# A four-layer graph network on one core: layers 1 to 3 as rounds of fixed order, and idle TensorE products in front of attention in layers 1 and 2

## The chip, the core and the metric

The kernel runs on one core of a Trainium2 chip. The metric is the device time of one execution in microseconds (us). TensorE is PE in the profile (PEld its weight loads), VectorE is DVE, ScalarE is ACT, GpSimd is POOL, SyncE is SP.

## The reference

There are 4096 nodes with 256 channels and a dense 0/1 adjacency matrix with about 9 neighbours a row, itself among them. Each of four layers adds an attention over a node's neighbours to the node's own row:

```python
h = np.maximum(layernorm(x), 0.0); x = x + L0(h)   # 8 heads, curvature bias, masked softmax
h = np.maximum(layernorm(x), 0.0); x = x + L1(h)   # 1 head: leaky_relu(a1.h_i + a2.h_j, 0.2)
h = np.maximum(layernorm(x), 0.0); x = x + L2(h)   # see below
h = np.maximum(layernorm(x), 0.0); x = x + L3(h)   # 4 heads of 64, see below
```

Layer 2 makes two softmaxes over the neighbours, of the scores e and of -e, applies both to `inp` (the second with a minus sign), concatenates the two results, multiplies them by `wtrans` (512x256) and applies elu. Layer 3 has dot-product scores `leaky_relu(h_n . h_m, 0.01)` per head; a pair that is not an edge has the score 1.0 instead of minus infinity, so that the softmax runs over all 4096 nodes, and the result goes through relu.

## The kernel before, in words

The nodes are 32 tiles of 128 rows. From the adjacency matrix the kernel builds, beside layer 0, a list of each tile's edges: 9 chunks (`EC`) of 128 slots, a slot holding the row number of one neighbour, and marks that say which of the tile's rows a slot belongs to. Layer 0 is ordered by a planner with due times; the change does not touch it.

For layers 1, 2 and 3 each layer first has a table in device memory (`table1`, `table2`, `table3`) with the transformed rows of all nodes, written two tiles at a time by `store_two` on ACT's DMA queue (L774). A tile's work in a layer is this:

- **Gather.** POOL issues one indirect DMA per chunk (L909) into one of 6 buffers `g` (`G`). Chunks 0 to 6 are early chunks (`gather_early`): they name only rows of tiles 0 to 27 and read only that part of the table, so that a layer's first gathers can start before the layer before has written its last four tiles. Chunk 7 is a late one (`gather_late`) and reads the whole table; in layer 2 chunk 8 is gathered in the same way. The tile's own rows (`SELF`) come by a DMA on SP's queue (L923).
- **Chunk 8 in layers 1 and 3** holds rows of tiles 28 to 31, and is not gathered: these four tiles' rows stay on the chip as three bf16 parts (`late_rows`, made by `keep_late`), and 12 products on PE pick from them (`expanded`, L1701).
- **Scores, weights, attention.** ACT makes exponentials and DVE multiplies the tile's 0/1 marks with them, giving the weight matrix `sw` (L1819 in layer 1, L1897 to L1906 in layer 2). PE sums the gathered rows with it (`summed`, L930, in layers 1 and 3; L1919, two halves of 14 products, in layer 2). In layer 3 the scores come from products of the marks with the tile's own rows (L2056), DVE multiplies them with the gathered rows (L2060), sums per head (L2061), and multiplies the rows with the weights (L2074); then `summed` uses the plain marks.
- **Afterwards.** Layer 1 adds the result to x, normalizes it and writes rows of `table2` (`finish1`, `rows2`). Layer 2 scales and transposes the two results (`signed2`, `turn_signed`), multiplies by `wtrans` (`through_wt`, L1954), applies elu, adds, normalizes (`finish2`), transposes (`turn3`), multiplies by layer 3's weights, and stores rows of `table3` and their three bf16 parts (`rows3`). Layer 3 divides, applies relu, adds and stores four tiles at a time.

The order comes from `run()` (L1714 on). Each step has a lag; the step of tile t with lag l is written down in round t + l. PE executes its instructions in exactly the order in which they are written down; for DVE, ACT, POOL and SP a scheduler chooses the order when the program is built. `begin` (the early gathers) has the lag 2 - G = -4. The late gathers of the first five tiles have lags of their own, so that at the start of a layer early gathers of four tiles come first, and `BEHIND` and `issue_after` keep POOL to this order:

```python
            def late_lag(t):
                return (-1, -2, -2, -3, -3)[t] if t < 5 else 2 - G
            steps = [(-3, loads), (2 - G, begin), (late_lag, begin_late)] + [
                (lag, lambda t, f=f: f(t, of[t])) for lag, f in steps
            ]
```

Of the kernel before, what the change touches and what calls it, by code (L numbers as in the profile page):

```python
# [20 lines left out]
P = 128  # L21
# [683 lines left out]
BEHIND = 3  # L705
ROW0, ROW1, ROW3 = C + H0 + CF, C + 2, C
# [7 lines left out]
def gnn_lists(  # L714
# [917 lines left out]
    with tc.tile_pool(name="work", bufs=2) as work, tc.tile_pool(name="kept", bufs=1) as kept:  # L1632
# [9 lines left out]
        mine1 = kept.tile([P, MINE, P + 3], BF16, name="mine1")  # L1642
        nc.gpsimd.tensor_copy(mine1[:, :, :P], ident_b[:, None, :].to_broadcast([P, MINE, P]))

        def by_edge(pool, t, st, own_t):

            my = mine1[:, t % MINE, :]
            nc.any.tensor_copy(my[:, P:], upper(own_t))
            s, parts = spread(pool.tile([P, 3, 512], F32, name="s_ps"), st, my, P + 3)
            a = work.tile([P, EC + 1], F32, name="a", bufs=3)  # L1650
            nc.vector.tensor_reduce(a[:, :EC].rearrange("p (b c) -> p b c", c=3), parts, AX.X, OP.add)
            return s, a
# [31 lines left out]
        def go_to(t, to):  # L1684

            pm = bank(ps_e, "pe")[:, :P]
            nc.tensor.matmul(
                pm, lhsT=col_late[:, t : t + 1].to_broadcast([P, P]), rhs=ident, start=True, stop=True
            )
            nc.vector.tensor_tensor(  # L1690
                to.rearrange("p (b e) -> p b e", b=LB), pm[:, None, :].to_broadcast([P, LB, P]),
                late_no[:, :, None].to_broadcast([P, LB, P]), op=OP.is_equal,
            )

        def expanded(t, of, width, pool, name):

            to = of.pop("to")
            ps = bank(pool, name)[:, :width]
            for b in range(LB):
                for i in range(3):  # L1700
                    nc.tensor.matmul(  # L1701
                        ps, lhsT=to[:, b * P : (b + 1) * P], rhs=late_rows[:, b, i, :width],
                        start=(b == 0 and i == 0), stop=(b == LB - 1 and i == 2),
                    )
            nc.scalar.copy(of["g"][:, LATE, :width], ps)
# [8 lines left out]
        def run(table, width, x_of, steps, first=None, expand=False, rows=True):  # L1714


            of, late = [{} for _ in range(NT)], {}

            def loads(t):
                two = t // 2 * 2  # L1720
                if t == two:
                    of[t]["ss"] = work.tile([P, 2, EC * P], BF16, name="ss", bufs=3)
                    if not first:
                        nc.sync.dma_start(of[t]["ss"], s_of[t // 2])
                of[t]["pair"] = of[two]["ss"]
                of[t]["s"] = by_slot(of[t]["pair"][:, t - two, :])
                if rows:
                    if t == two:
                        of[t]["sts"] = work.tile([P, 2, (EC + LB) * P], BF16, name="st", bufs=4)
                        if not first:  # L1730
                            nc.sync.dma_start(of[t]["sts"], rows_of[t // 2])
                    both = of[two]["sts"][:, t - two, :]
                    of[t]["st"], of[t]["to"] = both[:, : EC * P], both[:, EC * P :]
                if first:
                    marked(first, t, of[t]["st"])
                    go_to(t, of[t]["to"])
                    if t > two:
                        store(rows_of[t // 2], of[two]["sts"])
# [6 lines left out]
            def begin(t):  # L1745
                with ExitStack() as queue:
                    if t - BEHIND in late:
                        queue.enter_context(tc.issue_after(late.pop(t - BEHIND).ins))
                    of[t]["g"] = gather_early(t, table, width, g_pool)

            def begin_late(t):
                last = gather_late(t, of[t]["g"], table, width, range(EARLY, LATE if expand else EC))
                if t < G - BEHIND:
                    late[t] = last

            def late_lag(t):

                return (-1, -2, -2, -3, -3)[t] if t < 5 else 2 - G

            steps = [(-3, loads), (2 - G, begin), (late_lag, begin_late)] + [  # L1760
# [3 lines left out]
            for lag, f in steps:  # L1764
                for t in range(NT):
                    rounds.setdefault(t + (lag(t) if callable(lag) else lag), []).append((f, t))
            for r in sorted(rounds):
                for f, t in rounds[r] if r < NT else sorted(rounds[r], key=lambda s: -s[1]):
# [12 lines left out]
        with tc.tile_pool(name="only1", bufs=2) as only, tc.tile_pool(name="l1_o", bufs=2, space=PSUM) as ps_o, tc.tile_pool(  # L1781
# [10 lines left out]

            def expand1(t, of):
                expanded(t, of, ROW1, ps_e, "pe")

            def before1(t, of):
                s_ps, of["a"] = by_edge(ps_s, t, of["st"], own[0][:, t, :])
                nc.scalar.copy(three(of["s"]), s_ps)
                nc.scalar.copy(of["a"][:, SELF:], own[0][:, t, 0:1])
                if t % 2:  # L1800
                    store(s_of[t // 2], of["pair"])

            def give2(t, of):
                a, st = a2_of[:, t, :], of.pop("st")
                pm = bank(ps_m, "pm")[:, : EC * 3].rearrange("p (c s) -> p c s", c=EC)
                for c in range(EC):
                    nc.tensor.matmul(
                        pm[:, c, :], lhsT=st[:, c * P : (c + 1) * P], rhs=upper(own[1][:, t, :]),
                        start=True, stop=True,
                    )  # L1810
                nc.vector.tensor_reduce(a[:, :EC], pm, AX.X, OP.add)
                nc.scalar.copy(a[:, SELF:], own[1][:, t, 0:1])

            def weigh1(t, of):
                s = scores(of["g"], of.pop("a"))
                w = work.tile([P, EC + 1], F32, name="w")
                nc.scalar.activation(w, s, AF.Exp)
# [8 lines left out]
            def attend1(t, of):  # L1826
                sw, g = of.pop("sw"), of.pop("g")
                o = of["o"] = bank(ps_o, "o")[:, : C + 1]
                summed(o, sw, g, C + 1, [(sw[:, SELF, :], g[:, SELF, : C + 1])])

            def finish1(t, of):
# [7 lines left out]
                store_x(xs[1], t, of)  # L1839

            def rows2(t, of):
# [3 lines left out]
                for i, dst in enumerate((row[:, C + 1 :], own[1][:, t, 0:1])):  # L1845
# [3 lines left out]
                    )  # L1849
                if t % 2:  # L1850
                    store_two(table2, t, rows12[t // 2 % len(rows12)])
                split_own(own[1], t, 1)
# [4 lines left out]
                    (3, give2), (0, weigh1), (2, finish1), (1, attend1), (-1, before1),  # L1857
                    (2, rows2), (-1, expand1),
                ],
                first=only, expand=True,  # L1860
# [16 lines left out]
        with tc.tile_pool(name="only2", bufs=2) as only, tc.tile_pool(name="l2_o", bufs=2, space=PSUM) as ps_o, tc.tile_pool(  # L1877
# [5 lines left out]
            def weigh2(t, of):  # L1883

                s = scores(of["g"], a2_of[:, t, :])
                w = work.tile([P, EC + 1, 2], F32, name="w2")
                nc.scalar.activation(w[:, :, 0], s, AF.Exp)
                nc.scalar.activation(w[:, :, 1], s, AF.Exp, scale=-1.0)
                sw = of["sw"] = weights().rearrange("p (h c s r) -> p h c s r", h=2, s=2, r=HP)
# [22 lines left out]
            def attend2(t, of):  # L1912
                sw, g = of.pop("sw"), of.pop("g")
                of["o"] = []
                for h in range(2):
                    o = bank(ps_o, f"o{h}")[:, : C + 1]
# [6 lines left out]
                    of["o"].append(o)  # L1923

            def signed2(t, of):
                scale = small.tile([P, 2], F32, name="scale")
                two = of["two"] = only.tile([P, 2, C], F32, name="two")
                for h, o in enumerate(of["o"]):
                    nc.vector.reciprocal(inv[2][:, t, h : h + 1], o[:, :1])
# [3 lines left out]
                for h, o in enumerate(of.pop("o")):  # L1933
                    nc.scalar.activation(two[:, h, :], o[:, 1:], AF.Copy, scale=scale[:, h : h + 1])

            def turn_signed(t, of):
                two = of.pop("two")
                pt = bank(ps_t, "pt").rearrange("p (h k r) -> p h k r", h=2, k=KC)
# [3 lines left out]

                two_t = of["two_t"] = only.tile([P, 2, KC, 2, HP], F32, name="two_t")
# [13 lines left out]

            def finish2(t, of):
                pp, x = of.pop("pp"), of.pop("x")

                low = only.tile([P, C], F32, name="low")
                nc.vector.tensor_scalar(low, pp, 0.0, None, op0=OP.min)
                nc.scalar.activation(low, low, AF.Exp)
                nc.vector.scalar_tensor_tensor(low, pp, 0.0, low, op0=OP.max, op1=OP.add)
                nc.vector.scalar_tensor_tensor(x, low, -1.0, x, op0=OP.add, op1=OP.add)
                of["r"], of["rstd"] = normed(work, x)
                store_x(xs[2], t, of)
# [3 lines left out]
            def turn3(t, of):  # L1971
                of["hT"] = transposed(work, ps_t, of.pop("r"))

            def rows3(t, of):
                pp = times(ps_t, of.pop("hT"), w3_s, C)
                if t % 2 == 0:
# [4 lines left out]
                row, parts = (a[:, t % 2] for a in rows3_of)  # L1981
                nc.vector.scalar_tensor_tensor(
                    row, pp, of.pop("rstd"), b3_s, op0=OP.mult, op1=OP.add
                )
                if t % 2:
                    store_two(table3, t, rows3_of[0])
                    last3.append(rows3_of[0])
                rest = work.tile([P, C], F32, name="rest3")
                in_parts([parts[:, i, :] for i in range(3)], row, rest)
                if t % 2:  # L1990
                    store(own3[t // 2], rows3_of[1])
                nc.vector.tensor_add(all_rows, all_rows, row)
                sq = work.tile([P, D3], F32, name="sq")
                for k in range(K3):
                    nc.scalar.activation(
                        sq, row[:, k * D3 : (k + 1) * D3], AF.Square, accum_out=self3[:, t, k : k + 1]
                    )

# [3 lines left out]
                    (0, weigh2), (1, signed2), (2, finish2), (0, attend2), (2, turn3), (1, turn_signed),  # L2002
                    (2, rows3), (1, through_wt),
# [201 lines left out]
```

## Time and profile before

| | |
|---|---|
| median of 14 runs | 1612.54 us (1607.07 to 1617.04) |
| the profiled execution's own time | 1614.67 us |
| its span, first to last instruction | 1612.9 us |
| mean granted TensorE clock | 0.891 |
| busy: PE, DVE, ACT, POOL | 1289.6, 1148.0, 683.5, 1109.6 us |
| POOL's indirect DMAs | 1088, of which 288 in layer 0 |
| layer 1's gathers on POOL | from 530.03 us |
| layer 2's gathers | from 876.12 us |
| layer 3's gathers | 1249.85 to 1572.60 us |

A row of a timeline gives the start in us from the span's start, the duration, the engine, the line and operation, what it writes and reads, how many such were merged, and in brackets how long the engine had been idle and what released it. "ACTq" and "SPq" are DMA issues on those engines' queues. A row with several merged instructions gives the time from the first to the last. "issue" is idle time for which the profile shows no wait.

### The profile page before, as it was taken

The page shows a single profiled execution, that of the slowest core. Times are in us where ns is not written, and L with a number is a line of the kernel's source. Part 1 is how long each engine was busy: PE and PEld are TensorE (multiplying, and loading weights), DVE is VectorE, ACT ScalarE, POOL GpSimd, SP SyncE. Part 2 cuts the span into 40 slices and gives each one's busy share as a digit, 9 for nine tenths or more (in the row PEclk, how much of TensorE's full clock was granted, in tenths as well). Part 3 has the DMA queues.
Part 4 walks back from the last instruction along what each step waited for, and adds up shares of the span by engine and source line. Part 5 has one row for each costly group of instructions (what it writes and reads, how often), then busy time and mean ns, then how long its engine had stood idle before and what let it go on. Part 6 is the DMA issues. An engine that isn't in the chain of part 4 may idle for free.

```text
span 1612.9 us, 24838 instructions
## 1 busy us (share of the span) xinstructions
PE 1289.6 (80%) x7536; PEld 1032.9 (64%) x7536; DVE 1148.0 (71%) x3174; ACT 683.5 (42%) x1798; POOL 1109.6 (69%) x1179
## 2 busy tenths in 40 slices
PE   4673878877887679777777299988898789999995
PEld 2442655655665468665666288776777678888884
DVE  5666878888885567556555267666566599999995
ACT  4675767786452355434332044434334411211120
POOL 2127767776676677777777777777777777777770
PEclk9975888788998889888888599999999999999998
DMA  8978879997455668776768656666666667777740
GB/s 256 309 235 328 295 264 301 323 331 250 132 153 138 192 208 262 222 221 208 223 201 274 205 166 204 201 188 189 198 186 193 211 214 237 240 245 244 255 126 20
DMA packets 169888, 356.67 MB, mean 221 GB/s; under 512 B 32272, under 2 KB 104208, under 8 KB 169744
## 3 DMA queue, kind: packets, MB, share of 16 engines
q0 software_dynamic: 52224, 145.30, 32.4%
q1 hardware_dynamic: 67970, 143.98, 26.5%
q10 hardware_dynamic: 49550, 65.71, 11.4%
q8 instruction: 62, 1.02, 0.3%
q14 instruction: 82, 0.67, 0.1%
HBM read 291.66 MB, written 63.21 MB: 220 GB/s over the span
## 4 chain that ended last, share of the span: by engine, by line
PE 31%; DVE 17%; POOL 15%; DMA 11%; issue 9%; ACT 3%; DVEq 0%; ACTq 0%; POOLq 0%; SPq 0%
PE o L930 17%; POOL g L909 15%; DMA g<-table,nbr 10%; PE o L1919 4%; PE pv L2056 3%; DVE g L2074 2%; DVE sw L1897 2%; PE pv L1701 2%; PE pt L1954 2%; PE pt L874 1%; DVE g L1537 1%; PE pt L865 1%; DVE prod L1847 1%; DVE stats L842 1%; ACT mask L1204 1%
## 5 line engine op out<-in xcount | busy, mean ns | idle before, releaser
L909 POOL DMA_INDIRECT g<-table,nbr x1088 | 1080.2, 993 | 372.8 <-issue 295.9
L930 PE MATMUL o<-g,sw 128*128 128x257 f32 (+1 forms) x1216 | 313.5, 417 | 5.9 <-DVE sw L1822 5.9
L930 PEld LDWEIGHTS o<-g,sw 128*128 128x128 f32 x1216 | 252.6, 210 | 50.8 <-DVE sw L1822 6.6
L1919 PE MATMUL o<-g,sw 128*128 128x257 f32 x896 | 204.8, 386 | 27.0 <-issue 27.0
L1919 PEld LDWEIGHTS o<-g,sw 128*128 128x128 f32 x896 | 173.9, 194 | 53.8 <-issue 27.0
L930 PE MATMUL o<-g,s_f 128*128 128x264 f32 x576 | 152.8, 425 | 0.0
L930 PEld LDWEIGHTS o<-g,s_f 128*128 128x128 f32 x576 | 124.8, 217 | 27.5
L1204 ACT ACTIVATE mask<-adj,minus_half 128x1024 bf16<-128x1024 int32 x112 | 125.4, 1144 | 16.8 <-DMA adj<-in_adj_l 7.4
L2065 ACT ACTIVATE pm<-s 128x40 f32<-128x40 f32 x32 | 6.6, 208 | 227.2 <-DVE s L2063 219.9
L2056 PE MATMUL pv<-parts,st 128*128 128x256 bf16 x864 | 101.2, 275 | 1.4 <-DMA parts<-own 1.4
L2060 DVE TENSOR_TENSOR v<-pv,g 128x512 f32<-128x512 f32 (+1 forms) x160 | 90.7, 628 | 4.4 <-PE pv L2056 4.4
L2056 PEld LDWEIGHTS <-st 128*128 128x128 bf16 x864 | 85.1, 99 | 12.5 <-DMA parts<-own 1.8
L1954 PE MATMUL pt<-wt_s,two_t 128*128 128x256 f32 x256 | 69.5, 418 | 29.1 <-ACT two_t L1945 28.9
L2074 DVE SCALAR_TENSOR_TENSOR g<-pm,g 128x2560 f32<-128x2560 f32 x32 | 90.3, 2823 | 2.5 <-ACT g L2070 1.9
L1537 DVE TENSOR_TENSOR g<-g,pt 128x2560 f32<-128x2560 f32 x32 | 90.0, 2814 | 0.4 <-ACT pt L1534 0.3
L1701 PEld LDWEIGHTS <-st 128*128 128x128 bf16 x768 | 74.3, 98 | 13.8
L898 ACT ACTIVATE off<-place,minus 128x1152 bf16<-128x1152 f16 x64 | 80.0, 1249 | 6.6 <-DVE st L899 5.0
L2061 DVE TENSOR_REDUCE s<-v 128x36 f32<-128x2304 f32 x32 | 81.7, 2553 | 1.1
L865 PE MATMUL pt<-ident,r 128*128 128x128 f32 x192 | 42.8, 310 | 47.5 <-DVE r L845 35.7
L1954 PEld LDWEIGHTS pt<-wt_s,two_t 128*128 128x128 f32 x256 | 49.5, 203 | 45.9 <-ACT two_t L1945 39.6
L874 PE MATMUL pt<-wcat,hT 128*128 128x272 f32 (+1 forms) x256 | 73.2, 410 | 4.9 <-ACT hT L867 4.5
L1777 DVE TENSOR_TENSOR s<-g,a 128x10 f32<-128x10 f32 x32 | 5.5, 171 | 99.0 <-DMA g<-table,nbr 84.1
(360 smaller groups left out, 2285.3 us busy)
## 6 DMA issues: line engine op xcount, KB each, us to landing
adj<-in_adj_l SPq DMA_DIRECT2D x128, 512.0 KB
ss<-s_of SPq DMA_DIRECT2D x32, 576.0 KB
g<-table,nbr POOLq DMA_INDIRECT x1088
rows_of<-st ACTq DMA_DIRECT2D x16, 832.0 KB
st<-rows_of SPq DMA_DIRECT2D x16, 832.0 KB
x<-x SPq DMA_DIRECT2D x24, 512.0 KB
s_of<-ss ACTq DMA_DIRECT2D x16, 576.0 KB
table<-row ACTq DMA_DIRECT2D x32, 258.0 KB
```

What stands on the lines that cost most here:

```text
L874: nc.tensor.matmul(pp, lhsT=hT[:, k, :], rhs=w[:, k, :], start=(k == 0), stop=(k == KC - 1))
L909: last = nc.gpsimd.indirect_dma_start(out=g[:, c, :width], out_offset=None, in_=table[: NE if c < EARLY else N, :], in_offset=bass.Indirec ...
L930: nc.tensor.matmul(o, lhsT=a, rhs=b, start=(i == 0), stop=(i == len(pairs) - 1))
L1204: nc.scalar.activation(m, a, AF.Sign, bias=minus_half, scale=1.0)
L1537: nc.vector.tensor_mul(gh, gh, w[:, :, :, None].to_broadcast([P, K, H0, D0]))
L1701: nc.tensor.matmul(ps, lhsT=to[:, b * P : (b + 1) * P], rhs=late_rows[:, b, i, :width], start=(b == 0 and i == 0), stop=(b == LB - 1 and i ...
L1919: nc.tensor.matmul(o, lhsT=sw[:, h, i].rearrange("p s r -> p (s r)"), rhs=g[:, c, : C + 1], start=(i == 0), stop=(i == HC + 1),)
L1954: nc.tensor.matmul(pp, lhsT=lhs[:, k, :], rhs=wt_s[:, k, :], start=(k == 0), stop=(k == 2 * KC - 1))
L2056: nc.tensor.matmul(pv[:, k, :], lhsT=st[:, (a + k) * P : (a + k + 1) * P], rhs=parts[:, i, :], start=(i == 0), stop=(i == 2),)
L2060: nc.vector.tensor_mul(v[:, a : a + n, :], pv[:, :n, :], g[:, a : a + n, :C])
L2061: nc.vector.tensor_reduce(s[:, :EC, :], heads(v, K3), AX.X, OP.add)
L2074: weighed3[t] = nc.vector.scalar_tensor_tensor(gh, w[:, :, :, None].to_broadcast([P, K, K3, D3]), -math.e, gh, op0=OP.add, op1=OP.mult,)
```

## The change

It has three parts.

1. `run()` collects, for rounds 0 to 31, all DVE and all ACT instructions in the order in which they are written down, and chains them so (`in_order`). The scheduler no longer chooses their order there. The helpers are cut into smaller steps with lags of their own, so that a round names each engine's order in full.
2. `stir` writes 5 (layer 1) or 3 (layer 2) products of an identity with itself, bf16, 128x512, into the bank of the attention that follows. The attention's first product overwrites them.
3. In layer 3 the attention moves from lag 1 to lag 2. `lead`, the lag of the early gathers, is worked out from `last_use`; in layer 3 it becomes -3 (before: -4). In layers 1 and 2 it becomes -5, and the scores and weights move one round earlier as well. A few small operations change engine: relu and the scale of the own weight in layer 3 from DVE to ACT, some copies of one column from ACT to DVE.

```diff
+        def stir(to, n):
+            for _ in range(n):
+                nc.tensor.matmul(
+                    to, lhsT=ident_b, rhs=ident_b[:, None, :].to_broadcast([P, to.shape[1] // P, P]),
+                    start=True, stop=True,
+                )
+
+        def in_order(first):
+            traced = nc.cur_bb.bb.instructions
+            for engine in (nc.vector.engine, nc.scalar.engine):
+                mine = [i for i in traced[first:] if i.engine == engine]
+                for a, b in zip(mine, mine[1:]):
+                    tc.add_manual_dep(b, a.name, mybir.DependencyInfo(
+                        mybir.DependencyClass.NoSync, mybir.DependencyReason.DATA), reason="round")
...
-                return (-1, -2, -2, -3, -3)[t] if t < 5 else 2 - G
+                return first_use - 1 + t // 2 - t if t < 5 else lead
+            lead = last_use + 1 - G
...
             for r in sorted(rounds):
+                if r == 0:
+                    start = len(nc.cur_bb.bb.instructions)
+                if r == NT + 0:
+                    in_order(start)
...
@@ layer 1
-                    (3, give2), (0, weigh1), (2, finish1), (1, attend1), (-1, before1),
-                    (2, rows2), (-1, expand1),
+                    (-1, take1), (-1, score1), (0, attend1), (-3, go_to), (3, take2), (1, finish1),
+                    (2, store2), (-3, off1), (-1, weigh1), (-2, spread1), (-2, expand1), (-3, mark1), (-4, look_up),
+                    (2, give2), (1, rows2), (-3, keep_rows),
+                last_use=0, first_use=-1, rows=True,
@@ layer 1, attend1
+                stir(o, 5)
@@ layer 2, attend2, before its first half
+                    if h == 0:
+                        stir(o, 3)
@@ layer 2
-                    (0, weigh2), (1, signed2), (2, finish2), (0, attend2), (2, turn3), (1, turn_signed),
-                    (2, rows3), (1, through_wt),
+                    (-1, score2), (0, attend2(0)), (2, through_wt), (-1, weigh2), (1, signed2), (3, turn3),
+                    (3, take3), (0, attend2(1)), (4, row3), (2, low2), (1, turn_signed), (4, parts3), (2, finish2),
+                    (3, rows3), (1, take_signed),
+                last_use=0, first_use=-1, late=2, s=True,
@@ layer 2, what was the end of rows3
+            def row3(t, of):
...
                 row, parts = of["row"], of["parts"] = tuple(a[:, t % 2] for a in rows3_of)
+                nc.vector.scalar_tensor_tensor(
+                    row, of.pop("p3"), of.pop("rstd"), b3_s, op0=OP.mult, op1=OP.add
+                )
+                nc.vector.tensor_add(all_rows, all_rows, row)
                 if t % 2:
                     store_two(table3, t, rows3_of[0])
@@ layer 3
-                [(0, weigh3), (1, attend3), (-1, before3), (2, finish3), (-1, expand3), (-2, own_parts)],
+                    (-3, own_parts), (5, out3), (1, total3), (1, full3), (0, multiply3), (2, attend3),
+                    (0, score3), (0, exp3), (3, finish3), (4, add3), (-1, expand3), (-1, spread3),
+                    (-1, take3), (-1, last3_of), (0, weigh3),
+                last_use=2, first_use=0, s=True, rows=True,
@@ layer 3, finish3
-                nc.vector.tensor_mul(y, o[:, :C] by head, inv[3] by head)
-                nc.vector.scalar_tensor_tensor(x, y, 0.0, x, op0=OP.max, op1=OP.add)
+                for k in range(K3):
+                    nc.scalar.activation(
+                        y[:, k, :], o[:, k * D3 : (k + 1) * D3], AF.Relu, scale=inv[3][:, t, k : k + 1]
+                    )
```

In words for layer 2: `score2` and `weigh2` (lag -1) make a tile's weights one round ahead of its attention; `attend2(0)` and `attend2(1)` are the two halves; `through_wt` now has lag 2 and stands between them, with `turn3` (lag 3); `take_signed` and `take3` are the ACT copies that were inside `turn_signed` and `turn3`; `rows3` (lag 3) keeps the products; `row3` (lag 4) writes the rows and issues the store of `table3`; `parts3` (lag 4) makes the bf16 parts. In ACT's fixed order of a round the two scaled results of `signed2` come first, then `take3`, then the store of `row3`.

## Prediction

> **What bounds the kernel now.** I read the page first (engines, granted clock, costliest groups), then busy time by stage for layers 1, 2, 3 and the tail, then the POOL timeline across the layer borders, then ACT and PE there, and last the end of the chain of waits.
>
> The stages first; the columns are busy time (instructions) of PE, its weight loads, DVE, ACT, POOL, then the granted TensorE clock, the DMA share and GB/s.
>
> ```profile
> 530.00:876.00 346.00, 260.56 (x1676) 218.13 (x1675) 207.13 (x689) 142.32 (x345) 268.23 (x257) 0.86 0.74 226
> 876.10:1249.80 373.70, 314.24 (x1434) 259.60 (x1434) 221.65 (x636) 141.38 (x589) 286.00 (x288) 0.93 0.64 193
> 1249.80:1572.70 322.90, 304.38 (x1941) 254.54 (x1941) 297.11 (x414) 76.44 (x225) 243.35 (x256) 0.98 0.69 221
> ```
>
> POOL runs 256, 288 and 256 gathers here, one per chunk of each tile (8, 9, 8 per tile). POOL looks only 77% busy, yet it is the bound: a gather's row shows about 0.95 us and then 0.30 us of "issue", and nothing else fits between two of them.
>
> ```profile
> 1249.85 0.94 POOL L909 DMA_INDIRECT g<-table,nbr  x1 [0.30 <-PE o L1919]
> 1284.16 0.95 POOL L909 DMA_INDIRECT g<-table,nbr  x1 [0.30 <-issue]
> 1287.15 0.95 POOL L909 DMA_INDIRECT g<-table,nbr  x1 [2.04 <-issue]
> 1571.66 0.94 POOL L909 DMA_INDIRECT g<-table,nbr  x1 [0.30 <-issue]
> ```
>
> The first row is layer 3's first gather, on the heels of layer 2's last; the second is the last of the 28 early gathers of layer 3 that go ahead, the third its first late one, held 1.74 us beyond the usual 0.30 until the whole table of layer 3 is stored; the fourth is the last gather of all. So the stream never stops from 530.03 to 1572.60. At 1.25 us each, 256 gathers are 320 us; the stages last 346, 374 (360 for 288) and 323, and the excess is gathers that take longer than 0.95 us: 26.3 us in layer 1, 14.3 in layer 2, 1.9 in layer 3. Laid beside DVE's rows, nearly all of it falls under the multiplies L1819 and L1897 (bf16 marks times f32 weights).
>
> The border of layers 2 and 3 on ACT's queue: these are the table3 stores of tiles 26/27 and 30/31.
>
> ```profile
> 1245.72 0.37 ACTq L774 DMA_DIRECT2D table<-row  x1
> 1280.18 0.37 ACTq L774 DMA_DIRECT2D table<-row  x1
> ```
>
> The early gathers (chunks 0 to 6) read tiles 0 to 27 only, so they need the first of these stores; it was issued 4.1 us ahead of the gather at 1249.85, which did not wait. Layer 1's first gather, which did wait, started 3.66 us after its store. I take 3.9 us from issue to a start. The late gathers need the second store: 6.97 us passed there, behind other stores.
>
> The end:
>
> ```profile
> 1583.54 2.81 DVE L2060 TENSOR_TENSOR v<-pv,g 128x512 f32<-128x512 f32 x5
> 1586.38 2.55 DVE L2061 TENSOR_REDUCE s<-v 128x36 f32<-128x2304 f32 x1
> 1590.15 2.82 DVE L2074 SCALAR_TENSOR_TENSOR g<-pm,g 128x2560 f32<-128x2560 f32 x1
> 1593.03 0.86 PE L930 MATMUL o<-g,ident 128*128 128x260 f32 x2 [4.26 <-DVE g L2074]
> 1593.69 5.68 PE L930 MATMUL o<-g,sw 128*128 128x260 f32 x18
> 1600.55 0.38 ACTq L774 DMA_DIRECT2D out<-x  x1
> ```
>
> Tile 31's last gather ended at 1572.60 and lands some 2.5 us later, but its multiply starts at 1583.54: at the end compute is about 8.5 us behind POOL. In layer 3 DVE and PE are full (297 and 304 of 323) and tiles go by every 9.48 us, from tile 0 at about 1290. So layer 3 ends by compute, layers 1 and 2 by POOL.
>
> **The change, part by part.** The profiled execution took 1614.67 us, its span 1612.9; the median is 1612.54. I sum on the span and carry the difference to the median.
>
> *The idle products.* 5 of 128x512 bf16 before each attention in layer 1, 3 in layer 2. The nearest row is a 128x512 bf16 product at 0.38 to 0.39 us each, as latency; pipelined, by width from this trace's f32 products, about 0.21. So 0.64 to 1.2 us a tile in layer 2, 1.1 to 1.9 in layer 1. PE has 85 us idle in layer 1 (2.7 a tile) and 59 in layer 2 (1.9 a tile), so both fit. They hold PE warm: attention of one tile in layer 3 takes 4.65 us at clock 1.0 against 6.4 us for the last tile after 4.3 us of idling. But PE is not the bound in layers 1 and 2: price 0, except 0.64 on the path below. The Trainium skill ("TensorE: Matmul & The Clock Gate", Part 1) says that activity releases a throttled clock and an idle window of about 3.4 us restores it, which fits products put into such gaps. By that rule layer 1's clock rises from 0.86 towards 1, which would be 260.6 x 0.14 = 36 us if PE set its pace; by the rows POOL does, so the sum takes 0.
>
> *Order of rounds on DVE and ACT, layers 1 and 2.* The work is the same (a few one-column copies go from ACT to DVE). POOL's order in these layers does not move, and its buffers come free 35 us or more before a gather needs them. In layer 2 PE's round is 10.1 us by rows (attention 6.07, through_wt 1.9, turn3 0.38, turn_signed 0.60, rows3 1.13) plus 0.64 to 1.2, against POOL's 11.67: still hidden, and worth 0; if the cover were gone, 32 tiles would cost their excess each. The slow gathers stay since L1819 and L1897 stay. The Trainium skill ("SBUF — State Buffer", Who interferes with whom) says that DVE in a two-port mode shuts GpSimd out for a whole instruction, which speaks against moving copies to DVE. Here DVE's layer 3 (92% busy) costs the gathers only 1.9 us, so what harms is a few kinds of instruction, not a busy DVE; 64 copies of one column cannot weigh by either.
>
> At layer 1's end, store2 of tiles 26/27 moves behind round 29's exponentials, about 870; it becomes readable at 874 to 876, and POOL comes for it at 876.12. 0 to 2 us; I take 0.
>
> *The store of table3.* This is the term that decides. Before, rows3 of tile 27 has lag 2 and its store leaves as ACT gets to it (1245.72), beside the attention of tiles 29 and 30. Now row3 has lag 4, and in ACT's fixed order the store of tiles 26/27 stands in round 31, behind two(30) and take3(28). take3(28) waits for turn3(28) on PE, which stands behind the first half of attention of tile 31 and through_wt(29). That half waits for tile 31's weights, and those for layer 2's last gather. So layer 3's first gather now waits for layer 2's last tile. From rows: tile 31 landed at 1252.56 (row score); its weights are done at 1255.8 (L1897 to L1906). Then signed2(29) 0.6, two(29) 0.9, turn_signed(29) 0.6 and rows3(27) 1.13 with hops: 1259.3. Idle products 0.64, half an attention 3.04: 1263.0. through_wt(29) 1.9 (its operand is ready at about 1263): 1265.1; turn3(28) 0.38, hT 0.37: store at 1266.0. Plus 3.9: first gather at 1269.9 instead of 1249.85, 20 us of POOL standing still. Bounds: 10 us if only tile 31's weights and signed2(30) precede the store (1258.5, gather at 1262.4), 23 if the store lands as slowly as the other one (6.97).
>
> *POOL's order in layer 3.* Lead -3 for -4: three tiles' early chunks (21 gathers) stand before the first late one, not four. L0 then comes 26.3 us after the first gather: 1296.2. The whole table: tile 31's way through through_wt, finish2, turn3, rows3 takes about 10.2 us by rows after attention ends at about 1271, hops, then 6.97: 1289 to 1292. So no second wait. Had the store not been late, L0 would wait here: 1287.15 (before's time) plus the 235 gathers left instead of 228 is 8.8 us later by itself.
>
> *Layer 3's rounds.* DVE loses pm (0.29) and one of two 0.42 steps: 9.48 becomes about 9.0 to 9.1, below POOL's 10.0 for 8 gathers. Tile 0 at about 1299 plus 31 x 9.1 is 1581, before the last gather lands, so POOL now ends last. Stream: 322.75 - 1.74 = 321.0 from 1269.9: 1590.9, landed 1593.4. Then the last two multiplies 1.1, reduce 2.55, leaky 0.2, exponential with hops 0.65, weigh 2.82: 1600.7. Attention 6.4 (cold as now): 1607.1. finish3 now has four relus on ACT and an add: 1.9 where reciprocal, y and x took 1.1: 1609.0. From out's issue to the span's end 12.35: 1621.3.
>
> Sum: POOL +18.3 at its end, of which the present lag of compute takes back some 10, tail +0.3: span +8.4, median 1612.54 + 8.4 = 1621.
>
> **Rivals.**
> *Faster: the slow gathers shrink.* If the fixed order put L1819 and L1897 where they hurt less, up to 40.6 us could go. Every 1 us saved moves everything. From 8.4 us the gain breaks even, from 11.6 it shows. Half gone: 1601. Against: POOL gathers without a pause, so any place of the multiply meets some gather.
> *No change: the store is less late.* At the lower bound (gather at 1262.4) L0 could start at 1288.7, the table's end holds it to 1288 to 1292, and POOL is 1 to 4 us past break-even (first gather at 1261.5, L0 at 1287.8): 1613 to 1617.
> *Slower still: layer 2 ends late.* Tiles 4 to 11 run at 9.75 us, PE-bound, to work off 15.4 us of backlog. At 11.26 (rows, with products at 0.39) each tile recovers only 0.41 and some 4 us are left at tile 31; with 2 us at layer 2's start and 3 for a slower landing: 1630.
>
> **Numbers.** My case 0.62, less late 0.13, faster 0.12, slower still 0.13. This kernel's measurement tells about 0.2%, 3.2 us, from no change. Low 1609 (less late, a few slow gathers gone), high 1632 (all upper bounds of my case).
>
> **What would show it.** Right: POOL idle some 20 us before layer 3's first gather; the table3 store of 26/27 within 2 us of 1266, behind hT; 0.30 before L0; layer 3 tiles every 10.0; multiply(31) right after its last landing. Granted clock up in layer 1 with its stage still 346. Wrong: the first gather before 1262, layer 1 or 2 shorter by over 5 us, or layer 3's DVE round above 9.6.

## The result, and the profile after

The changed kernel takes 1634.8 us (median of 10 runs, 1626.8 to 1641.51), the kernel before 1611.49 us (median of 47). The ratio is 1.014, 95% interval 1.0125 to 1.0156: slower by 23 us. Forecast were 1621 us and a range up to 1632: the direction and its main cause hold, the size does not. The profiled execution took 1634.93 us, its span is 1632.9 against 1612.9.

The stages of the changed kernel first, cut where POOL's streams of gathers begin and end; the columns are those of the stages before.

```profile
529.00:874.30 345.30, 286.21 (x1829) 223.79 (x1828) 228.69 (x728) 137.84 (x302) 267.60 (x257) 0.90 0.73 222
879.80:1255.00 375.20, 323.64 (x1510) 261.23 (x1509) 211.78 (x629) 135.30 (x560) 287.68 (x288) 0.93 0.62 185
1276.20:1599.10 322.90, 300.79 (x1944) 253.38 (x1943) 285.23 (x347) 107.53 (x365) 243.58 (x256) 0.96 0.68 217
```

Each stage is as long as before within 2 us: 345, 375 and 323 us. The idle products raise layer 1's granted clock from 0.86 to 0.90 and its PE time by 26 us, and the stage does not move. What is new lies between the stages. POOL's timeline of the changed kernel, at the start of layer 2, at that of layer 3, and at layer 3's first late gathers:

```profile
879.81 0.94 POOL L910 DMA_INDIRECT g<-table,nbr  x1 [5.60 <-DMA table<-row]
1276.22 0.94 POOL L910 DMA_INDIRECT g<-table,nbr  x1 [21.29 <-PE o L1992]
1304.19 0.94 POOL L910 DMA_INDIRECT g<-table,nbr  x1 [0.81 <-issue]
1307.76 0.94 POOL L910 DMA_INDIRECT g<-table,nbr  x1 [1.38 <-issue]
1598.09 0.94 POOL L910 DMA_INDIRECT g<-table,nbr  x1 [0.30 <-issue]
```

Before, the first two waits were 0.30 us each. POOL now stands 5.6 us before layer 2 and 21.3 before layer 3, and its last gather ends at 1599.04 instead of 1572.61. The first table store that each of these waits for, on ACT's queue (tiles 26/27 of table2 and of table3):

```profile
870.86 0.38 ACTq L775 DMA_DIRECT2D table<-row  x1
1273.23 0.37 ACTq L775 DMA_DIRECT2D table<-row  x1
```

From issue to the gather's start the first took 8.95 us and the second 2.99. Two windows of the changed kernel around the first; the last two columns are the busy share of the DMA engines and GB/s:

```profile
863.00:871.00 8.00, 8.00 (x38) 6.52 (x37) 4.00 (x19) 2.05 (x5) 6.17 (x7) 0.68 0.95 312
871.00:880.00 9.00, 6.09 (x39) 4.68 (x37) 2.85 (x11) 1.85 (x4) 2.79 (x4) 1.00 1.00 376
```

The trace names PE's attention of tile 31 as the releaser of the second wait, since its end is the last event before the gather. It is not what the gather needs: in e5 below, on POOL and PE, the gather starts before that attention's second half.

```profile
1263.47 0.94 POOL L910 DMA_INDIRECT g<-table,nbr  x1 [14.86 <-PE o L1992]
1265.14 3.20 PE L1992 MATMUL o<-g,sw 128*128 128x257 f32 x14
```

What the gather follows is the store: 2.99 us after it here, 2.98 in e1 and e5, 2.99 in e7. What the store itself stood behind, on DVE, PE and ACT of the changed kernel:

```profile
1260.42 0.17 DVE L1784 TENSOR_TENSOR s<-g,a_of 128x10 f32<-128x10 f32 x1 [5.91 <-DMA g<-table,nbr]
1267.99 3.20 PE L1992 MATMUL o<-g,sw 128*128 128x257 f32 x14
1271.02 1.89 PE L2034 MATMUL pt<-wt_s,two_t 128*128 128x256 f32 x8
1272.75 0.38 PE L2056 MATMUL pt<-ident,r 128*128 128x128 f32 x2
1273.17 0.37 ACT L2060 COPY hT<-pt 128x256 f32<-128x256 f32 x1 [2.35 <-PE pt L2056]
```

This is the chain of the prediction, link by link: tile 31's gathers land (score at 1260.42), half of its attention, through_wt of tile 29, turn3 of tile 28, the copy hT, and then the store.

The tail of the changed kernel, with tile 31's exponential, its weights, and the two last attentions of layer 3 behind one another:

```profile
1604.84 0.21 ACT L2175 ACTIVATE pm<-s 128x40 f32<-128x40 f32 x1 [5.03 <-DVE s L2171]
1605.34 0.92 ACT L2208 ACTIVATE y<-o,inv 128x64 f32<-128x64 f32 x4
1605.44 2.83 DVE L2184 SCALAR_TENSOR_TENSOR g<-pm,g 128x2560 f32<-128x2560 f32 x1 [0.23 <-ACT pm L2176]
1606.31 1.23 PE L931 MATMUL o<-total_s,ident 128*128 128x260 f32 x2 [4.34 <-ACT y L2208]
1608.20 6.08 PE L931 MATMUL o<-g,sw 128*128 128x260 f32 x18
1615.00 4.11 PE L931 MATMUL o<-g,sw 128*128 128x260 f32 x18
```

Attention of tile 30 waited, with PE idle for 4.34 us, until the relus of tile 28 (L2208) had freed its bank; ACT's fixed order puts them behind tile 31's exponential. Tile 31's weights were ready at 1608.3, but PE was busy until 1614.1.

### The profile page after: what moved, and what is told of

Read it like the earlier page. It is cut to its first block, busy times and chain, and to the rows that moved or that the text cites. A ratio compares the mean times of both kernels' runs of the same rounds, so it can differ in the third digit from the quotient of the medians.

```text
span 1632.9 us, 25449 instructions
## 1 busy us (share of the span) xinstructions
PE 1334.9 (82%) x7792; PEld 1049.9 (64%) x7792; DVE 1146.9 (70%) x3158; ACT 715.3 (44%) x1910; POOL 1109.7 (68%) x1179
## 3 DMA queue, kind: packets, MB, share of 16 engines
q1 hardware_dynamic: 67970, 143.98, 25.9%
q10 hardware_dynamic: 49550, 65.71, 11.6%
## 4 chain that ended last, share of the span: by engine, by line
PE 22%; POOL 21%; DVE 18%; DMA 11%; issue 10%; ACT 4%; ACTq 0%; DVEq 0%; POOLq 0%; SPq 0%
POOL g L910 21%; PE o L931 12%; DMA g<-table,nbr 10%; PE pv L2140 2%; PE o L1992 2%; DVE sw L1967 2%; DVE g L1538 1%; PE pv L1685 1%; DVE stats L843 1%; PE pt L875 1%; DVE sw L1869 1%; DVE r L846 1%; DVE st L1807 1%; DMA g<-table 1%; DVE s L2170 1%
## 5 line engine op out<-in xcount | busy, mean ns | idle before, releaser
L931 PE MATMUL o<-g,sw 128*128 128x257 f32 (+1 forms) x1216 | 295.3, 399 | 19.6 <-DVE sw L1872 19.6
L931 PEld LDWEIGHTS o<-g,sw 128*128 128x128 f32 x1216 | 241.0, 200 | 71.8 <-DVE sw L1872 31.6
L1992 PEld LDWEIGHTS o<-g,sw 128*128 128x128 f32 x896 | 170.1, 193 | 52.3 <-DVE sw L1967 24.9
L2140 PE MATMUL pv<-parts,st 128*128 128x256 bf16 x864 | 104.9, 280 | 3.2 <-ACT g L2154 1.9
L2140 PEld LDWEIGHTS <-st 128*128 128x128 bf16 x864 | 86.8, 100 | 17.0 <-issue 4.3
L1685 PEld LDWEIGHTS <-st 128*128 128x128 bf16 x768 | 76.0, 101 | 29.8 <-issue 14.9
L837 ACT ACTIVATE rstd<-mv,eps 128x1 f32<-128x1 f32 (+1 forms) x104 | 30.6, 294 | 121.5 <-DVE mv L844 105.5
L1784 DVE TENSOR_TENSOR s<-g,a_of 128x10 f32<-128x10 f32 x32 | 5.5, 171 | 97.7 <-DMA g<-table,nbr 97.1
L1701 PE MATMUL o<-ident_b 128*128 128x512 bf16 x256 | 73.1, 412 | 1.2 <-DVE x L1886 0.6
L866 PE MATMUL pt<-ident,r 128*128 128x128 f32 x128 | 30.0, 323 | 44.5 <-DVE r L846 31.1
L2010 ACT ACTIVATE two<-o,scale 128x256 f32<-128x256 f32 x64 | 27.0, 471 | 89.2 <-DVE scale L2006 89.2
```

The lines of the kernel that those rows point to most:

```text
L931: nc.tensor.matmul(o, lhsT=a, rhs=b, start=(i == 0), stop=(i == len(pairs) - 1))
L1685: nc.tensor.matmul(ps, lhsT=to[:, b * P : (b + 1) * P], rhs=late_rows[:, b, i, :width], start=(b == 0 and i == 0), stop=(b == LB - 1 and i ...
L1701: nc.tensor.matmul(to, lhsT=ident_b, rhs=ident_b[:, None, :].to_broadcast([P, to.shape[1] // P, P]), start=True, stop=True,)
L1992: nc.tensor.matmul(o, lhsT=sw[:, h, i].rearrange("p s r -> p (s r)"), rhs=g[:, c, : C + 1], start=(i == 0), stop=(i == HC + 1),)
L2140: nc.tensor.matmul(pv[:, k, :], lhsT=st[:, c * P : (c + 1) * P], rhs=parts[:, j, :], start=(j == 0), stop=(j == 2),)
```

## Experiments

Theory: POOL's gathers set the pace, and the loss is POOL standing still because table stores leave late, plus the tail. Rivals: the idle products cost time; the fixed order slows the layers themselves; layer 3's new form is slower.

**The idle products taken out (e1), and put in alone (e2).**

```diff
-                stir(o, 5)
-                    if h == 0:
-                        stir(o, 3)
```

> The changed kernel without the idle TensorE products. Theory (late stores: POOL stands still before layer 2 and layer 3 because the table stores leave late): within 3 us of the changed kernel, 1632 to 1637 us, POOL still stands 19 to 21 us before layer 3; granted clock in layers 1 and 2 lower by a few hundredths. Rival (the idle products take PE time that the tiles need): 1615 to 1625 us, the stop before layer 3 shorter by 10 us or more. Rival (they are needed to keep the clock up): slower than the changed kernel by 5 us or more.

1633.37 us, ratio to the kernel before 1.0112 (1.0076 to 1.0148); POOL stood 20.93 us before layer 3, and layer 1's granted clock was 0.87. The reverse, the kernel before plus these lines:

> The kernel before, with the idle products alone (5 in layer 1, 3 in layer 2). Theory (POOL bounds layers 1 and 2, PE has 1.9 to 2.7 us idle a tile): within 3 us of the kernel before, 1609 to 1615 us, at a granted clock in layer 1 above 0.86. Rival (they take PE time that is needed): 1620 us or more. Rival (a warm clock is worth time): 1605 us or less.

1616.68 us, ratio 1.0017 (1.0001 to 1.0033): some 3 us slower by the medians, 0 to 5 by the interval, at clock 0.90 in layer 1. The products cost little and bring nothing; the rivals on them fall. The changed kernel without them still loses 20 of the 23 us by the medians.

**Layer 3 alone (e3).** Layers 1 and 2 as before, layer 3 with the changed steps, order and lead.

```diff
-            run(table3, ROW3, xs[2], [(0, weigh3), (1, attend3), ...], expand=True)
+            run3(table3, ROW3, xs[2], [(-3, own_parts), (5, out3), ...], last_use=2, first_use=0, ...)
```

> The kernel before, with the changed kernel's layer 3 alone (rounds of fixed order, lead -3), layers 1 and 2 as before. Theory (late stores): no stop before the first gather of layer 3; the first late gather waits for the whole table until about 1287 us with 21 instead of 28 gathers ahead of it, some 9 to 11 us of POOL standing; the last gather ends near 1581 us instead of 1572.6, and the compute that was 8.5 us behind catches up: 1610 to 1616 us, about as before. Rival (layer 3's fixed order is itself slower): 1625 us or more.

1614.7 us, ratio 1.0005 (0.9987 to 1.0023). POOL went from layer 2 to layer 3 without a stop and then stood at the first late gather, on its timeline:

```profile
1288.21 0.94 POOL L909 DMA_INDIRECT g<-table,nbr  x1 [11.02 <-issue]
```

The last gather ended at 1583.18, near the 1581 expected, and the faster rounds of layer 3 paid for it. So layer 3 by itself is not the loss: the 20 us between this and the changed kernel come with layers 1 and 2 and the borders behind them.

**The same with four tiles ahead (e4).**

```diff
-            steps = [(-3, loads), (lead, begin), ...
+            steps = [(-3, loads), (lambda t: lead - (t < G), begin), ...
```

> As the run before it, but the first six tiles' early gathers one round earlier, so that four tiles' early chunks stand before the first late one, as in the kernel before. Theory: POOL's stream as in the kernel before (last gather ends near 1572.6 us), tiles of layer 3 no longer lag behind it; the tail from the last gather to the end is that of the changed kernel, 33.9 us: 1604 to 1609 us. Rival (layer 3's fixed order is itself slower): 1615 us or more.

1608.81 us, ratio 0.9971 (0.995 to 0.9992): a little faster than the kernel before. The wait at the first late gather fell to 2.89 us; the last gather ended at 1578.43, though, not near the 1572.6 expected.

**The fixed order in layer 3 alone (e5).** Steps and lags of the changed kernel stay.

```diff
-                if r == NT + 0:
+                if r == NT and s is not None and rows:
                     in_order(start)
```

> The changed kernel with the fixed order of DVE and ACT in layer 3 alone; in layers 1 and 2 the steps and their lags stay, but the scheduler chooses the order. Theory (the store of table3 waits for layer 2's last tile because ACT's and DVE's fixed order puts it there): the store of tiles 26/27 then stands behind the results of tile 30 only, some 10 us earlier; the stop before layer 3 is 9 to 13 us instead of 21, the stop before layer 2 under 4: 1619 to 1626 us. Rival (the later lags alone, row3 4 rounds behind, make the stops): within 3 us of the changed kernel, 1632 to 1638.

1622.41 us, ratio 1.0047 (1.002 to 1.0073). No stop before layer 2; 14.86 us before layer 3, a little above the 9 to 13 expected. Without the order 12 of the 23 us are back by the medians, 15 by the ratios: 6.4 at layer 3's stop, 5.3 at layer 2's. The larger part of layer 3's stop, 14.86 us, comes with the lags, the order aside.

**Layer 2's round in another order (e6).**

```diff
-  (-1, score2), (0, attend2(0)), (2, through_wt), (-1, weigh2), (1, signed2), (3, turn3),
-  (3, take3), (0, attend2(1)), (4, row3), (2, low2), (1, turn_signed), (4, parts3), (2, finish2),
-  (3, rows3), (1, take_signed),
+  (1, signed2), (0, attend2(0)), (2, through_wt), (2, low2), (2, finish2), (3, turn3),
+  (3, take3), (-1, score2), (-1, weigh2), (0, attend2(1)), (1, turn_signed), (1, take_signed),
+  (3, rows3), (3, row3), (3, parts3),
```

> The changed kernel, layer 2's round written in another order: signed2, low2 and finish2 ahead of score2 and weigh2, and row3 with its store one round earlier (lag 3) directly behind rows3. Everything else, the fixed order too, stays. Theory: the store of tiles 26/27 waits for tile 31's weights, but not for its attention, some 8 us earlier; the stop before layer 3 is 11 to 14 us, that before layer 2 stays near 5.5: 1624 to 1629 us. Rival (layer 2 itself is slowed by the fixed order): no faster than 1632 us.

1623.88 us, ratio 1.0062 (1.0041 to 1.0084). The order stays fixed, and 11 us are back with layer 2's round rewritten and its store a round earlier: the store left 3.7 us after tile 31's score instead of 12.8. The stop before layer 2 was 6.85 us, where some 5.5 were expected. POOL's timeline of this run at layer 3's start:

```profile
1272.55 0.94 POOL L910 DMA_INDIRECT g<-table,nbr  x1 [12.32 <-DVE x L2046]
```

**Layer 1's store one round earlier (e7).**

```diff
-                    (2, store2), (-3, off1), ...
-                    (2, give2), (1, rows2), (-3, keep_rows),
+                    (-3, off1), ...
+                    (2, give2), (1, rows2), (1, store2), (-3, keep_rows),
```

> The changed kernel with layer 1's store of table2 one round earlier (lag 1, directly behind rows2). Theory: the stop of 5.6 us before layer 2 falls to 0 to 2 us, all else as in the changed kernel, the stop before layer 3 too: 1629 to 1632 us. Rival (POOL is late there for another reason, as the transfers that fill the DMA engines): the stop stays above 4 us, 1633 to 1637 us.

1631.41 us, ratio 1.0105 (1.0068 to 1.0143). The stop before layer 2 is gone, that before layer 3 stays (20.21 us). Layer 1's stream of gathers took 347.7 us instead of 345.1, so 3.4 us are won by the medians and not the whole stop. POOL's timeline of this run at layer 2's start:

```profile
875.55 1.29 POOL L910 DMA_INDIRECT g<-table,nbr  x1 [0.30 <-ACT row L1895]
```

**The tail (e8).** e4, with finish3 first in its round.

```diff
-  (-3, own_parts), (5, out3), (1, total3), (1, full3), (0, multiply3), (2, attend3),
-  (0, score3), (0, exp3), (3, finish3), (4, add3), ...
+  (-3, own_parts), (5, out3), (3, finish3), (1, total3), (1, full3), (0, multiply3), (2, attend3),
+  (0, score3), (0, exp3), (4, add3), ...
```

> The kernel before with the changed kernel's layer 3 and four tiles of early gathers ahead (1608.8 us measured), and finish3 (reciprocal and four relus) written first in layer 3's round instead of behind exp3. Theory (at the end attention of tile 30 waits for a bank that tile 28's relus free, and these stand behind the last exponential): attention of tile 30 no longer waits for it and is over before tile 31's weights are ready; the tail from the last gather to the end goes from 33.5 to 29 to 30 us: 1603 to 1606 us. Rival (the two last attentions run one after the other anyway): 1608 us or more.

1607.86 us, ratio 0.996 (0.9938 to 0.9982), the fastest version here. The tail from the last gather to the end went from 33.48 to 29.71 us, as expected; but this time the first late gather waited longer, on POOL's timeline of this run, and the sum is only 1 us better than e4, short of the 1603 to 1606 expected:

```profile
1293.35 0.94 POOL L909 DMA_INDIRECT g<-table,nbr  x1 [5.37 <-issue]
```

**One more gather a tile in layer 1 (e9)**, into a tile that nobody reads.

```diff
                     of[t]["g"] = gather_early(t, table, width, g_pool)
+                    if first:
+                        spare = first.tile([P, ROW1], F32, name="spare", bufs=2)
+                        nc.gpsimd.indirect_dma_start(out=spare[:, :width], ..., ap=nbr[:, t, 0:1], axis=0))
```

> The kernel before with one more gather per tile in layer 1: chunk 0 once more, into a tile that nobody reads. Nothing else on PE, DVE or ACT. Theory (POOL's gathers bound layers 1 and 2): 32 more gathers of 1.25 us, +38 to +42 us, 1651 to 1657 us. Rival (PE, DVE or the waits between them set the pace and POOL has room): +15 us or less.

1658.16 us, ratio 1.027 (1.0216 to 1.0323): 46 us more for 32 gathers, a little above the 40 expected, since they also wait 11.3 us for their own two buffers. Work added to POOL comes out in full: POOL is the bound there. (The gathers load the DMA engines too, but these were 66% busy from 530 to 883 us of this run.)

**Five tiles ahead (e10), and all remedies together (e11): two misses.**

```diff
-            steps = [(-3, loads), (lambda t: lead - (t < G), begin), ...
+            steps = [(-3, loads), (lambda t: lead - 2 * (t < G), begin), ...
```

> As e8 (1607.86 us), with the early chunks of five tiles instead of four ahead of layer 3's first late gather: 35 gathers, 43.9 us, which reach past the time at which the whole table is stored (1293 us in e8). Theory: the stop of 5.4 us before the first late gather goes, and as POOL ends last, the end comes 4 to 6 us earlier: 1602 to 1605 us. Rival (tile 0 can start no earlier, and compute of 9 us a tile then ends last): 1606 to 1609 us.

1619.18 us, ratio 1.0031 (1.0004 to 1.0058): slower than e8 by 11 us. Not five tiles but six went ahead: with this lag tile 5's early chunks were no longer held behind a late gather. 42 gathers stood before the first late one, tile 0's last multiplies came at 1306.03 instead of 1297.08, and at 9.15 us a tile from there compute ended last; POOL then waited 15.69 us for a buffer. The rival's mechanism is what happened, and by more.

> The changed kernel with the four remedies together: store2 one round earlier (e7), layer 2's round in the order of e6, five tiles of early gathers ahead in layer 3, finish3 first in its round (e8). Theory (the loss is the sum of these places): 1634.8 less 3.4, 10.9, 2 for the waits at the first late gathers and 4 for the tail: 1612 to 1617 us, and POOL's stop before layer 3 is still 11 to 13 us. Rival (a place is missing from the account): 1620 us or more.

1632.65 us, ratio 1.0123 (1.007 to 1.0177), above both expectations. Its places by the trace: 0.30 us before layer 2, 10.97 before layer 3, tail 29.5, as the theory has them; but it carries the same six tiles ahead, and layer 3's stream takes 337.5 instead of 322.8 us. Two remedies also give something back: the streams of layers 1 and 2 take 347.9 and 378.0 us here (345.1 and 375.1 in the changed kernel), as layer 1's does in e7 and layer 2's in e6 (377.8). POOL's timeline of this run:

```profile
1339.65 0.94 POOL L910 DMA_INDIRECT g<-table,nbr  x1 [17.32 <-issue]
```

**The sum with four tiles ahead (e12), and one transfer moved (e13): not settled.** e12 is e11 with `lead - 1` for the first six tiles. e13 is the changed kernel with the last store of marks moved:

```diff
-                    (2, give2), (1, rows2), (-3, keep_rows),
+                    (2, give2), (1, rows2), (lambda t: 0 if t == NT - 1 else -3, keep_rows),
```

> As e11, but with four tiles of early gathers ahead of layer 3's first late gather. In e11 the scheduler put all six tiles' early chunks there, 14 gathers more than in e8, which made tile 0 late and POOL wait 17.3 us for its buffers. Theory (the loss is the sum of the named places): no stop before layer 2, 11 us before layer 3, no long wait at gather 48; last gather near 1584 us, tail 29.5 us: 1612 to 1618 us. Rival (a place is missing from the account): 1622 us or more.

> The changed kernel with one transfer moved: the last 832 KB store of marks (tiles 30 and 31, issued at 863.0 us, 7.9 us ahead of table2's store) goes out three rounds later. Theory (table2's store took 8.95 us to become readable because the DMA engines were full): 1 to 2.5 us less from that store to layer 2's first gather, the stop before layer 2 at 3 to 4.6 us instead of 5.6 to 6.9. Rival (the landing is slow by itself, or what comes behind the store crowds it): 5.6 us or more.

These two, and their repeats (e14, e16 and e18 of e12's kernel, e15 and e17 of e13's), ran where the kernel before itself takes 2046 to 2070 us. There POOL stands more than 1 us, mostly 2 to 3, at some 17 to 26 places in each of the three layers, and the stops before layers 2 and 3 are 17 to 49 us. e12's kernel has ratios of 1.0129, 1.0092 and 1.0091 there, and in e16 one of 1.0198 with an interval too wide to use (1.0129 to 1.0267); e13's has 1.0139 in the repeat with an interval. A stop that depends on a store's landing can't be compared between the two, so neither question is answered: no run shows that all remedies together win back the sum of the places.

## Why the prediction was right or wrong

The direction, the main term and its chain were right; the sum was 11.6 us short on the span. Three of its terms failed: the stop before layer 2, taken as nothing (5.3 us more came), the landing of tile 31 (3.0 us taken, 5.5 came), and the tail, where one attention was counted and two ran (30.4 and 33.9). By its own steps, from the trace:

| step | predicted, us | measured, us | adds |
|---|---|---|---|
| layer 1's first gather | 530.03 | 529.06 | -1.0 |
| layer 1's stream | 345.8 | 345.1 | -0.7 |
| stop before layer 2 | 0 to 2, taken as before (0.30) | 5.60 | +5.3 |
| layer 2's stream | 373.4 | 375.1 | +1.7 |
| its last gather to tile 31's score | 3.0 | 5.5 | +2.5 |
| score to table3's store | 13.4 | 12.8 | -0.6 |
| store to first gather | 3.9 | 2.99 | -0.9 |
| layer 3's stream | 321.0 | 322.8 | +1.8 |
| last gather to the end | 30.4 | 33.86 | +3.5 |

- **The store of table3, right.** 20 us of standing were forecast, 21.29 came (21.0 more than before), and e5 and e6 show the cause: the same lags without the fixed order give 14.86, the fixed order with an earlier store 12.32. Both parts of the change count, and neither run brings back the 0.30 of before. That 20 came so near is in part luck: tile 31's landing took 2.5 us more, the chain to the store and the store's landing 1.5 less. The store left 7.2 us after the 1266 that the prediction named, mostly by the terms ahead of it in the table. The lower bound of "10 us" was a slip, since a gather at 1262.4 stands 12.5 us behind 1249.85; e6, in which the store waits for tile 31's weights but not for its attention, has 12.32.
- **"0 to 2 us; I take 0" at layer 1's end, the largest error.** The store was issued at 870.86, as forecast ("about 870"). The 3.9 us from issue to a start was wrong there: 8.95 us passed. I carried a latency from two quieter borders to one where other transfers were in flight; the DMA share was 0.95 and 1.00 around it (863 to 871 and 871 to 880 us). e7 shows that a store 8.4 us earlier removes the stop. The DMA packets in the traces show where the time went: the store's 256 packets ran from 2.3 to 7.2 us after its issue, and from the issue to the last of them 271 packets of gathers and 378 of SP's transfers (2.4 MB) ran too, while at layer 3's start the 256 packets of the other store ran from 0.9 to 1.8 us with no other transfer's beside them. e1 and e6 have the same lateness (8.49 and 9.14 us, the last packet at 6.9 and 7.7). No comparable run takes these transfers away, so that the store would then land in 3 us is not shown.
- **Tile 31's landing, mis-sized.** I took 3.0 us from the last gather to the score; it took 5.5. Two stores of 384 and 512 KB left ACT 0.7 and 0.25 us before that gather was issued, which the fixed order puts there. The packets of that last gather ended 5.5 us after its issue, beside 918 KB of these stores; in e6 and e11, which have no store there, they ended at 2.4 us, in e5 with one of the two at 3.5, in e7 with both at 4.2. No run moves these stores alone.
- **The tail, mis-sized.** "Attention 6.4 (cold as now)" counted one attention. With attend3 at lag 2 and two banks, tile 30's waited for tile 28's relus, and the two ran after one another: 10.8 us from tile 31's weights to the end of its attention. e8, with these relus written first, shows it: 3.8 us less tail than in e4.
- **"So no second wait" at L0 (layer 3's first late gather), nearly right**: waits of 0.81 and 1.38 us there and two gathers on, 0.5 and 1.1 beyond the usual 0.30.
- **The idle products at 0, right**: within some 3 us in both directions (e1, e2). They took 0.38 us each as latency. Layer 1's granted clock rose from 0.86 to 0.90, not close to the 1 that the prediction worked out, and the stage kept its length.
- **Slow gathers stay, right**: the excess over 0.945 us is 25.2, 15.5 and 1.7 us a layer, where the same count gives 25.9, 13.8 and 1.4 before. The rival that they would shrink falls. The rival of a late layer 2 named a time near the measured one (1630), but not its cause: it had PE leave 4 us at layer 2's end, and layer 2's stream grew by 1.7.
- **Layer 3's rounds of 9.0 to 9.1 us, right, though the two steps named for it (0.29 and 0.42) give 8.8**: a tile every 9.08 us where POOL does not hold it (multiplies at 1441.94, 1451.02 and 1460.09). The present lag of compute was taken back, as said; e4 turns that into a small gain (ratio 0.9971).
- The rest, 2 us between 11.6 and the 13.8 by medians, is the profiled execution of before, which stood 2.1 us above its median, while that of the changed kernel stands on it.

The upper end failed because its cases were stacked from layer 2's rounds and the landing of one store, while the stop before layer 2 was bounded at 2 us (5.6 came), and tile 31's landing and the tail were given no upper bound at all.

## What to carry to other kernels

When a stream crosses a barrier between stages (here gathers that read the table which the stage before writes), the last writes are on the critical path, however idle their engine: look where each engine's order puts exactly these stores before fixing an order or adding a round of lag. Cost a store by its landing beside the transfers of that moment, not by one at a quiet place. And when a pipeline gets deeper, count its last tiles by hand: banks and fixed order can set two of them behind one another.

## What the runs showed of the hardware

The 160 idle products of layer 1 raised PE's granted clock there from 0.86 to 0.90 and no more, though PE's busy time rose by 18 (e2, 530 to 870 us) to 26 us. A table store of 256 packets of about 1 KB needed 2.98 to 2.99 us from issue to the first reader's start at layer 3's start in four runs (the changed kernel, e1, e5, e7), where no other transfer's packets ran beside its own. With others beside it the same store needed 4.41 us in e4, 4.78 in e8, 5.28 in e11 and 5.49 in e6, and that of layer 1 8.49 to 9.14 us at layer 2's start (the changed kernel, e1, e6). A single packet took about 47 ns in all of these; what grew is the time before the first one and between them.
